# The seam between the first and second SAGE pass of a graph network: the last turn moved, norm and weights moved into the pass, memory laid out anew, graph 0 unpacked in one go

## The chip, the cores and the metric

One core of a Trainium2 chip runs the whole program in one launch. The metric is device time in microseconds, the median of several runs. Times inside the program are counted from the start of the profiled span. Engines are named as in the profile: PE (TensorE matmul), PEld (its weight loads), DVE (VectorE), ACT (ScalarE), POOL (GpSimd), SP (the engine that issues most DMAs here).

## The reference: what is computed

Sixteen graphs (B = 16) of 1024 nodes with 128 features each, and one adjacency matrix per graph.

```
x = layernorm(x + gated_graph_network(x, adj))        # layer 0: four rounds of aggregation and a GRU cell
adj_d = dilate(adj)                                   # row by row, drops some neighbours
# layer 1: three SAGE passes, each over all 16 graphs, with a batch norm over all graphs between them
def sage(x, Wr, Wx, b):
    agg = adj_d @ x / max(deg, 1)
    out = agg @ Wr + x @ Wx + b
    return out / max(norm(out), 1e-12) * mask
h1 = bn(relu(sage(x,  Wr1, Wx1, b1)))
h2 = bn(relu(sage(h1, Wr2, Wx2, b2)))
h3 = bn(relu(sage(h2, Wr3, Wx3, b3)))
x  = layernorm(x + concat(h1, h2, h3) @ Wl + bl)
```

The batch norm takes mean and variance over all 16 graphs. So pass two cannot form its weights before the last graph of pass one is through: the norm's scale is folded into the weights of the next pass, its shift into a bias row.

## The kernel before

Layer 0 and the dilation run up to about 1275 us, pass one (class Sage, function first) from there to 1704, pass two (second) to about 1949, pass three (third) and the end (last) to 2125.5.

**How a pass is staged.** A graph's work is cut into slots, 16 in pass one (slot, L1735) and 8 in pass two (slot_second, L1930). In each slot the code issues instructions for several graphs on all engines; the order of the code is the order on each engine, since the passes stand in a manual schedule. A graph's 1024 nodes are two halves f = 0 and 1 of 512. For a half, PE forms the output from aggregated features and the features themselves (pass one: out_first, L1705, banks p_oa and p_ob; pass two: out_next, L1907, banks q_oa and q_ob); DVE scales and adds (scale_rows, L1415 and L1416); ACT takes squares for the row norm (squares, L1423 and L1424); DVE makes the normalised rows s_r (rows, L1444 to L1449); ACT and POOL split them into a high and a low part (split, L1464 and L1465); PE turns them, four transposes into a PSUM tile s_tr (turned, L1470), ACT copies the tile out to s_rt and DVE takes its statistics (turn_r, L1732 and L1733). PE also aggregates the split rows with the adjacency (pass one: agg, L1696, banks p_ag; pass two L1954, banks q_ag), ACT copies the sums out to s_ag (evict, L1702), and SP stores s_rt and s_ag to DRAM, from where the next pass loads them.

**The last slots of graph 15 in pass one.** The turns of the halves stand in slots 11 and 13, the aggregation of the second half's high and low part in slots 12 and 14, the stores of the turned halves in slots 13 and 15 (L1832). The PSUM pool p_ps1, in which s_tr lies, has one buffer for each name.

**The seam.** run (L2161) calls first; then weights(1) (L1350): batch_norm (L1326 to L1331: statistics joined on DVE, a square root on ACT, four small DVE steps), three scaled weights (L1334: wr2, and the two halves of wxp), the shift as columns of beta (L1361), three matrix products for six bias rows in the PSUM tile s_v6 (L1362 to L1364, two matmuls each) and their split into three bf16 parts in r6 (parts, L1341 to L1348, eight DVE steps). Then it opens the pool of the accumulator acc (one tile for all graphs) and the pool s_ahead with three tiles s_rho, which POOL sets to zero (L2172), and calls second. There SP loads graph 0 (load_layer, L1877 and L1878: the sums q_agi, the turned features q_xt, the rows s_rho; load_second, L1887: acc; load_bytes, L1892: the first half of the adjacency, one byte for each entry), stores the two s_ag of graph 15 (L1865), and the slots begin. The load of the second half's bytes stands in slot 3.

**Unpacking.** The adjacency of pass two is cast from bytes to the matmul's type before it is used (unpack, L1895): eight casts for a graph, of 128x1024 each, one in a slot, four for the first half (tile q_at0) and four for the second (q_at1), on POOL, ACT, POOL, DVE in turn (L1903 for ACT, L1905 for the others). They begin in slot 3 of a graph and end in slot 2 of the next.

Memory comes from pools in a stack: a pool that is opened takes the addresses that a closed one left.

Of the kernel before, what the change touches and what calls it, by code (L numbers as in the profile page):

```python
# [1206 lines left out]
class Sage:  # L1207
# [191 lines left out]
    def start_half(self, b):  # L1399

        acc = self.acc[:, b, 4:, :]
# [333 lines left out]
    def slot(self, b, t):  # L1735
# [36 lines left out]
        if True:  # L1772
# [25 lines left out]
            if t in (11, 13):  # L1798
                self.turn_r(0, b, t // 13, self.ps1)
# [25 lines left out]
        if True:  # L1825
# [5 lines left out]
            if t in (13, 15):  # L1831
                nc.sync.dma_start(self.rt[b, t // 15], g["rt", t // 15])  # L1832
# [17 lines left out]
    def second(self):  # L1850

        nc, tc = self.nc, self.tc
        with ExitStack() as c:
# [27 lines left out]
    def load_second(self, b):  # L1881
# [5 lines left out]
        nc.sync.dma_start(self.acc[:, b], self.x1[b])  # L1887
# [7 lines left out]
    def unpack(self, b, t):  # L1895
# [5 lines left out]
        e = "gpsimd scalar gpsimd vector".split()[t % 4]  # L1901
# [5 lines left out]
    def out_next(self, b, f, ps):  # L1907
# [3 lines left out]
        for i in range(4):  # L1911
            blk = slice(i * P, (i + 1) * P)
            nc.tensor.matmul(pa[:, i, :], g["agi"][:, f, blk], self.wr2, start=True, stop=True)  # L1913
        for i in range(4):
# [15 lines left out]
    def slot_second(self, b, t):  # L1930
        nc, g, p = self.nc, self.g.get(b), self.g.get(b - 1)
        acc = lambda b, f: self.acc[:, b, 4 * f:4 * f + 4, :]
        if b < B:
# [5 lines left out]
            if t == 3:  # L1939
# [41 lines left out]
        if t >= 3:  # L1981
            if b < B:
                self.unpack(b, t - 3)
        elif p is not None:
# [10 lines left out]
    def third(self):  # L1995

        nc, tc = self.nc, self.tc
        with ExitStack() as c:
# [10 lines left out]
            for i in range(len(units) + 5):  # L2009
# [34 lines left out]
                if i < len(units):  # L2044
                    g["ss", f] = self.shared_squares(g["o", f])
                    acc = self.acc[:, b, 4 * f:4 * f + 4, :]
# [5 lines left out]
    def last(self):  # L2052
        nc, tc, cst = self.nc, self.tc, self.cst
        with ExitStack() as c:
# [12 lines left out]
            def half(b, f):  # L2067
# [6 lines left out]
                pp, acc = self.banks[b][f], self.acc[:, b, 4 * f:4 * f + 4, :]  # L2074
# [7 lines left out]
            def finish(b, f):  # L2082
                pp, acc = self.banks[b][f], self.acc[:, b, 4 * f:4 * f + 4, :]
# [77 lines left out]
    def run(self):  # L2161
        tc, nc = self.tc, self.nc
        self.first()
        with tc.tile_pool(name="s_psw", bufs=1, space=PSUM) as ps:
            self.weights(1, ps.tile([6, C], F32, name="s_v6"))
        accp = self.ctx.enter_context(tc.tile_pool(name="s_acc", bufs=1))
        self.acc = accp.tile([P, B, NB, C], F32, name="s_acc")
        self.rt_kept = self.late[:, :HF]
        self.ahead = self.ctx.enter_context(tc.tile_pool(name="s_ahead", bufs=1))
        self.rhos, self.layers = [self.ahead.tile([P, N], BF, name=f"s_rho{i}") for i in range(3)], 0  # L2170
        for t in self.rhos:
            nc.gpsimd.memset(t, 0.0)  # L2172
# [102 lines left out]
```

## Time and profile before

| | us |
|---|---|
| median of 3 runs | 2126.41 |
| the runs | 2126.14, 2126.41, 2129.80 |
| the profiled execution | 2127.28 |
| its span, first to last instruction | 2125.5 |
| PE busy in the span | 2050.1 (96%) |
| DVE, POOL, ACT busy | 1782.1, 1351.5, 1304.0 |
| mean granted clock of TensorE | 0.992 |

Busy time is an average over stages. What is of interest here is one short stretch, and in such a stretch the chain of waits tells more than shares do: which instruction ended last, what released it, and so on back.

### The profile page before, as it was taken

To read this page: it belongs to the slowest core of one execution; us is meant where nothing else is said; L and a number is where in the kernel's file an instruction comes from. 1 tells how busy PE (TensorE), PEld (TensorE's weight loads), DVE (VectorE), ACT (ScalarE), POOL (GpSimd) and SP (SyncE) were. 2 spreads that over 40 slices of the span, in tenths; PEclk is the share of its full clock that TensorE was granted. 3 is DMA by queue.
4 is the path that set the end of the run, shared out by engine and by line. 5 is a ranking of instruction groups with operands and counts; after the bars stand their busy time and mean duration, and the time that the engine had idled before them with its cause. 6 is when DMAs were issued, how large, how long until landed. Compare 5 with 4: busy or idle time off the path is not lost.

```text
span 2125.5 us, 32964 instructions
## 1 busy us (share of the span) xinstructions
PE 2050.1 (96%) x10218; PEld 1435.8 (68%) x10219; DVE 1782.1 (84%) x4090; ACT 1304.0 (61%) x3127; POOL 1351.5 (64%) x1459
## 2 busy tenths in 40 slices
PE   7999999999999999999999998999999989999997
PEld 4566556665655666556655656888888778888875
DVE  4898998988998988998889997888888767776876
ACT  3657557567466566565665655776677645555756
POOL 5458558557558468467466557777777545565866
PEclk9999999999999999999999998999999999999998
DMA  8348356348447457546367337888788589996515
GB/s 254 89 105 251 92 129 219 79 121 243 92 109 231 89 142 207 103 136 199 77 207 174 77 117 267 300 293 294 292 290 293 180 309 341 343 339 209 161 41 161
DMA packets 234896, 406.68 MB, mean 191 GB/s; under 512 B 79058, under 2 KB 101236, under 8 KB 234708
## 3 DMA queue, kind: packets, MB, share of 16 engines
q1 hardware_dynamic: 190388, 285.17, 40.5%
q0 software_dynamic: 41616, 117.98, 20.8%
q8 instruction: 83, 1.36, 0.3%
q10 hardware_dynamic: 2704, 1.31, 0.2%
q14 instruction: 105, 0.86, 0.1%
HBM read 314.00 MB, written 109.25 MB: 199 GB/s over the span
## 4 chain that ended last, share of the span: by engine, by line
PE 66%; DVE 16%; ACT 5%; issue 5%; DMA 4%; POOL 3%; SPq 0%; ACTq 0%; DVEq 0%; POOLq 0%
PE h_g L1104 18%; PE h_g L1092 13%; PE p_ag L1696 11%; PE q_ag L1954 5%; PE q_ob L1916 5%; DVE f_rank L737 4%; PE q_oa L1913 3%; DVE f_a L729 2%; PE p_u L1607 2%; PE s_tr L1470 2%; DMA h_a<-in_adj_dram 1%; PE h_g L1038 1%; DVE f_x L894 1%; ACT s_junk L1423 1%; DVE h_r L1116 1%
## 5 line engine op out<-in xcount | busy, mean ns | idle before, releaser
L1104 PE MATMUL h_g<-h_ms,h_wi 128*128 128x512 f32 x768 | 392.2, 592 | 0.0
L737 DVE TENSOR_TENSOR_SCAN f_rank<-f_a,f_first,f_pd 128x1024 f16<-128x1024 bf16 x128 | 299.4, 2345 | 4.2
L1092 PE MATMUL h_g<-h_a,h_hi 128*128 128x512 f32 x1024 | 278.2, 413 | 0.4 <-DMA h_a<-in_adj_dram 0.2
L1104 PEld LDWEIGHTS h_g<-h_ms,h_wi 128*128 128x128 f32 x768 | 145.5, 190 | 184.3 <-issue 168.9
L1092 PE MATMUL h_g<-h_a,h_lo 128*128 128x512 f32 x1024 | 262.1, 393 | 0.1
L1627 POOL CAST p_b<-p_at 128x512 uint8<-128x512 f32 x256 | 208.0, 834 | 80.6 <-DVE p_at L1619 42.4
L1092 PEld LDWEIGHTS h_g<-h_a,h_hi 128*128 128x128 f32 x1024 | 190.1, 188 | 60.5 <-issue 22.0
L1092 PEld LDWEIGHTS h_g<-h_a,h_lo 128*128 128x128 f32 x1024 | 189.6, 188 | 39.2 <-DVE h_lo L1031 1.1
L1123 POOL TENSOR_TENSOR h_zh<-h_r,h_h 128x512 f32<-128x512 f32 x64 | 82.3, 1286 | 199.1 <-ACT h_r L1119 196.1
L1104 PE MATMUL h_g<-h_h,h_wh 128*128 128x512 f32 x384 | 198.1, 597 | 3.3 <-DVE h_r L1116 3.3
L1104 PE MATMUL h_g<-late,h_wh 128*128 128x512 f32 x384 | 198.1, 597 | 0.7 <-DVE h_r L1116 0.7
L1119 ACT ACTIVATE h_r<-h_r,h_bi 128x512 f32<-128x512 f32 x128 | 92.4, 722 | 150.1 <-DVE h_r L1118 150.1
L1124 POOL TENSOR_TENSOR h_zh<-h_z,h_zh 128x512 f32<-128x512 f32 x128 | 165.6, 1294 | 10.0
L1095 ACT COPY h_ms<-h_g 128x512 f32<-128x512 f32 x128 | 73.7, 576 | 149.0 <-PE h_g L1092 148.8
L1423 ACT ACTIVATE s_junk<-s_o 128x128 bf16<-128x128 f32 x256 | 76.1, 298 | 128.6 <-DVE s_o L1416 128.6
L910 ACT ACTIVATE f_u<-f_rank,f_q 128x128 f16<-128x128 f16 (+7 forms) x128 | 110.5, 867 | 69.9 <-DVE f_rank L850 68.8
L1123 POOL TENSOR_TENSOR h_zh<-h_r,late 128x512 f32<-128x512 f32 x64 | 94.5, 1476 | 57.1 <-ACT h_r L1119 56.9
L2185 DVE SCALAR_TENSOR_TENSOR p_a<-p_a 128x1024 bf16<-128x1024 f32 x96 | 128.9, 1343 | 0.0
L778 POOL TENSOR_SCALAR_AFFINE_SELECT f_both<-f_both 128x512 bf16<-128x512 bf16 x32 | 20.6, 642 | 164.6 <-DVE f_both L777 164.6
L1916 PE MATMUL q_ob<-s_wxp,q_xt 128*128 128x256 f32 x512 | 121.7, 381 | 0.0
L887 ACT ACTIVATE f_pd<-f_rank,f_q 128x128 f32<-128x128 f16 x128 | 59.1, 462 | 98.9 <-DVE f_q L701 95.7
L1619 DVE SCALAR_TENSOR_TENSOR p_at<-p_nr,p_u 128x128 fp32r<-128x128 bf16 (+1 forms) x192 | 102.8, 543 | 19.9 <-ACT p_at L1611 15.4
(314 smaller groups left out, 5184.5 us busy)
## 6 DMA issues: line engine op xcount, KB each, us to landing
h_a<-in_adj_dram POOLq DMA_DIRECT2D x128, 512.0 KB, 9.3
p_a<-in_adj_dram SPq DMA_DIRECT2D x96, 512.0 KB
f_a<-in_adj_dram POOLq DMA_DIRECT2D x128, 256.0 KB, 6.3
e_nr<-f_nr SPq DMA_DIRECT2D x128, 256.0 KB
p_nr<-e_nr SPq DMA_DIRECT2D x32, 1024.0 KB
s_at<-p_b SPq DMA_DIRECT2D x32, 512.0 KB
s_ag<-s_ag SPq DMA_DIRECT2D x64, 256.0 KB
q_agi<-s_ag SPq DMA_DIRECT2D x32, 512.0 KB
```

The source lines that it names most:

```text
L737: nc.vector.tensor_tensor_scan(out, a, other[:, 0, 0:1].to_broadcast([P, N]), start, op0=ALU.add, op1=ALU.bypass)
L910: nc.scalar.activation(u[:, :n1], rank[:, g, :n1], AF.Abs, bias=q[:, 1, g:g + 1], scale=q[:, 0, g:g + 1])
L1092: nc.tensor.matmul(pm[f], part[:, j, :], st.adj[j][:, half[f]], start=(j == 0 and n == 0), stop=(j == NB - 1 and n == 1))
L1104: nc.tensor.matmul(pg, lhs, rhs, start=(i == 0), stop=(i == len(mm) - 1))
L1123: aid.tensor_tensor(d, r, h, ALU.subtract)
L1124: aid.tensor_tensor(d, z, d, ALU.mult)
L1619: self.nc.vector.scalar_tensor_tensor(g["at", f][:, j, :low], v[:, j, c0:c0 + low], 0.0, pu[:, :low], op0=ALU.is_lt, op1=ALU.is_lt)
L1627: self.nc.gpsimd.tensor_copy(g["b", f][:, j, :], g["at", f][:, j, :].bitcast(F32))
L1696: self.nc.tensor.matmul(pa, hi[:, j, :], at[:, j, :], start=(start and n == 0), stop=(stop and n == len(js) - 1))
L1916: nc.tensor.matmul(pb[:, i], g["xt"][:, f, blk], self.wxp, start=(i % 2 == 0), stop=False)
L1954: nc.tensor.matmul(p["pa", f], part[:, j, :], p["at", f][:, j, :], start=(t in (1, 4) and j == 0), stop=(t in (2, 5) and j == NB - 1))
L2185: nc.vector.scalar_tensor_tensor(junk, a, 0.0, a, op0=ALU.is_gt, op1=ALU.not_equal, accum_out=bad[:, c:c + 1])
```

## The change

- In pass one, for graph 15 alone, the turn of the second half moves from slot 13 to slot 12, ahead of that slot's aggregation; the stores of the turned halves move from slots 13 and 15 to slots 12 and 13.
- Right after that turn stands second_weights: batch norm, scaled weights and beta. wr2 is scaled as soon as the scale is there; beta's memset and copies go from DVE to POOL.
- The bias rows (three products and their split) are formed in pass two, in the first out_next, between the matmuls into q_oa and those into q_ob; their PSUM tile is one of s_tr.
- The pool s_ahead opens before that of acc; acc is 16 tiles, not one. In second four tiles (two q_rl, two s_rt) are taken from the pool q_wk ahead of all others and not used at that place; later tiles of these names take their turn.
- The first s_rho is set to zero before graph 0's loads, the other two between POOL's casts.
- The bytes of both halves of graph 0 are loaded at once, and its eight casts stand ahead of the slots: the first half's four on ACT, the second's four on POOL. The slots of graph 0 issue no casts.

```diff
-    def batch_norm(self, l):
+    def batch_norm(self, l, early=False):
...
         nc.vector.tensor_mul(ab[:, 0:1], ab[:, 0:1], vt[:, 3 * l + 1:3 * l + 2])
+        if early:
+            self.scaled(self.wr2, self.wr[:, l + 1, :], l)
         nc.vector.tensor_mul(mv[:, 0:1], mv[:, 0:1], ab[:, 0:1])
...
     def weights(self, l, v):
-        if l:
+        if l == 1:
+            beta = self.beta
+        elif l:
             self.batch_norm(l - 1)
...
+        if l:
             nc.tensor.matmul(v, beta[:, 0, :], self.wr[:, l, :], start=True, stop=False)
...
+    def second_weights(self):
+        nc, l = self.nc, 1
+        self.beta = beta = self.small.tile([C, 2, 6], F32, name="s_beta")
+        nc.gpsimd.memset(beta, 0.0)
+        self.batch_norm(0, True)
+        for i in range(2):
+            nc.gpsimd.tensor_copy(beta[:, i, 3 * i:3 * i + 3], self.ab[0][:, 1:2].to_broadcast([C, 3]))
+        self.scaled(self.wxp[:, 0, :], self.wx[:, 1, :], 0)
+        self.scaled(self.wxp[:, 1, :], self.wl[:, 0, :], 0)
...
-            if t in (11, 13):
-                self.turn_r(0, b, t // 13, self.ps1)
+            slots = (11, 12) if b == B - 1 else (11, 13)
+            if t in slots:
+                self.turn_r(0, b, slots.index(t), self.ps1)
+                if (b, t) == (B - 1, 12):
+                    self.second_weights()
...
-            if t in (13, 15):
-                nc.sync.dma_start(self.rt[b, t // 15], g["rt", t // 15])
+            slots = (12, 13) if b == B - 1 else (13, 15)
+            if t in slots:
+                nc.sync.dma_start(self.rt[b, slots.index(t)], g["rt", slots.index(t)])
...
+            for i in range(2):
+                self.wk.tile([P, NB, C], FR, name="q_rl")
+                self.wk.tile([C, HF], F32, name="s_rt")
+            nc.gpsimd.memset(self.rhos[0], 0.0)
             self.load_second(0)
-            self.load_bytes(0, 0)
+            for f in range(2):
+                self.load_bytes(0, f)
             for f in range(2):
                 nc.sync.dma_start(self.ag[B - 1, f], last["ag2"][f])
+            for f in range(2):
+                for t in range(4):
+                    self.unpack(0, 4 * f + t, ("scalar", "gpsimd")[f])
+                    if f == 1 and t in (1, 3):
+                        nc.gpsimd.memset(self.rhos[t // 2 + 1], 0.0)
...
             nc.tensor.matmul(pa[:, i, :], g["agi"][:, f, blk], self.wr2, start=True, stop=True)
+        if self.layers == 1:
+            self.weights(1, self.ps1.tile([P, 4, P], F32, name="s_tr")[:6, 0, :])
...
-            if t == 3:
+            if t == 3 and b:
                 self.load_bytes(b, 1)
...
-            if b < B:
+            if 0 < b < B:
                 self.unpack(b, t - 3)
-        elif p is not None:
+        elif b > 1:
             self.unpack(b - 1, t + 5)
...
         self.first()
-        with tc.tile_pool(name="s_psw", bufs=1, space=PSUM) as ps:
-            self.weights(1, ps.tile([6, C], F32, name="s_v6"))
-        accp = self.ctx.enter_context(tc.tile_pool(name="s_acc", bufs=1))
-        self.acc = accp.tile([P, B, NB, C], F32, name="s_acc")
-        self.rt_kept = self.late[:, :HF]
         self.ahead = self.ctx.enter_context(tc.tile_pool(name="s_ahead", bufs=1))
         self.rhos, self.layers = [self.ahead.tile([P, N], BF, name=f"s_rho{i}") for i in range(3)], 0
-        for t in self.rhos:
-            nc.gpsimd.memset(t, 0.0)
+        accp = self.ctx.enter_context(tc.tile_pool(name="s_acc", bufs=1))
+        self.acc = [accp.tile([P, NB, C], F32, name=f"s_acc{b}") for b in range(B)]
+        self.rt_kept = self.late[:, :HF]
         self.second()
```

More of the change, by code (lines that the diff above doesn't have):

```diff
@@ L1399, in start_half @@
     def start_half(self, b):
-        acc = self.acc[:, b, 4:, :]
+        acc = self.acc[b][:, 4:, :]
         self.head_banks(b)
@@ L1886, in load_second @@
         g = self.g[b]
-        nc.sync.dma_start(self.acc[:, b], self.x1[b])
+        nc.sync.dma_start(self.acc[b], self.x1[b])
     def load_bytes(self, b, f):
@@ L1893, in load_bytes, with unpack @@
             self.g[b]["b", f] = t
-    def unpack(self, b, t):
+    def unpack(self, b, t, e=None):
         nc, g, f, j = self.nc, self.g[b], t // 4, 2 * (t % 4)
@@ L1900, in unpack @@
         dst, src = g["at", f][:, j:j + 2, :], g["b", f][:, j:j + 2, :]
-        e = "gpsimd scalar gpsimd vector".split()[t % 4]
+        e = e or "gpsimd scalar gpsimd vector".split()[t % 4]
         if e == "scalar":
@@ L1931, in slot_second @@
         nc, g, p = self.nc, self.g.get(b), self.g.get(b - 1)
-        acc = lambda b, f: self.acc[:, b, 4 * f:4 * f + 4, :]
+        acc = lambda b, f: self.acc[b][:, 4 * f:4 * f + 4, :]
         if b < B:
@@ L2045, in third @@
                     g["ss", f] = self.shared_squares(g["o", f])
-                    acc = self.acc[:, b, 4 * f:4 * f + 4, :]
+                    acc = self.acc[b][:, 4 * f:4 * f + 4, :]
                     self.late = acc, pb[:, :, 1, :], acc
@@ L2073, in half @@
                         self.head_banks(b)
-                pp, acc = self.banks[b][f], self.acc[:, b, 4 * f:4 * f + 4, :]
+                pp, acc = self.banks[b][f], self.acc[b][:, 4 * f:4 * f + 4, :]
                 for i in range(4):
@@ L2082, in finish @@
             def finish(b, f):
-                pp, acc = self.banks[b][f], self.acc[:, b, 4 * f:4 * f + 4, :]
+                pp, acc = self.banks[b][f], self.acc[b][:, 4 * f:4 * f + 4, :]
                 for i in range(4):
```

## The prediction

> **What bounds the kernel now.** I read the span in stages first: busy time of each engine in each stretch. Columns: stretch and its length, then busy us (instructions) of PE, PEld, DVE, ACT, POOL, then the granted clock, the DMA share and GB/s.
>
> ```profile
> 1305.80:1704.00 398.20, 391.50 (x2930) 322.20 (x2929) 322.42 (x841) 272.40 (x784) 282.32 (x300) 1.00 0.76 274
> 1704.00:1723.80 19.80, 12.70 (x75) 10.41 (x74) 13.04 (x34) 6.19 (x24) 6.00 (x6) 0.91 0.83 300
> 1723.80:1949.00 225.20, 222.16 (x1262) 189.06 (x1263) 170.37 (x324) 124.88 (x409) 131.21 (x94) 1.00 0.92 321
> ```
>
> The two passes are bound by PE (391.5 of 398.2 us and 222.2 of 225.2). The seam between them is the 19.8 us from 1704.0 to 1723.8, in which no engine is full: there a chain decides. So I read the chain of work that ended last in that stretch (start, length, what):
>
> ```profile
> 1704.16 0.83 POOL s_rho L2172
> 1704.99 3.54 DMA q_agi<-s_ag
> 1708.54 0.49 issue
> 1709.03 2.05 PE q_oa L1913 x8
> 1711.07 2.25 PE q_ob L1916 x8
> ...
> 1713.59 0.70 DVE s_o L1416
> ...
> 1714.44 1.29 ACT s_junk L1423 x8
> ...
> 1720.68 1.63 POOL q_rl L1465
> 1722.31 1.45 POOL q_at L1905
> ```
>
> The reader sees, after the last aggregation of pass one: load of graph 0's sums, its output matmuls, then norm, and at the end POOL's cast of the adjacency bytes, for which PE stands still. Last I read the timeline of single engines for the steps that the change touches:
>
> ```profile
> 1699.22 0.60 PE L1470 MATMUL s_tr<-ident,s_r 128*128 128x128 f32 x4
> 1699.65 2.11 PE L1696 MATMUL p_ag<-p_at,p_rh 128*128 128x512 f32 x8
> ...
> 1723.81 2.18 PE L1954 MATMUL q_ag<-q_at,q_rh 128*128 128x512 f32 x8 [1.85 <-POOL q_at L1905]
> ```
> ```profile
> 1699.86 0.59 ACT L1732 COPY s_rt<-s_tr 128x512 f32<-128x512 f32 x1 [0.26 <-PE s_tr L1470]
> ...
> 1720.93 1.05 ACT L1903 CAST q_at<-q_b 128x1024 fp32r<-128x1024 uint8 x1
> 1721.88 0.62 ACT L1464 CAST q_rh<-s_r 128x512 fp32r<-128x512 f32 x1
> ```
>
> PE waits 1.85 us for POOL before pass two's first aggregation, at 1723.81; its transposes before that ended at 1721.32 + 0.63 = 1721.95, and matmuls overlap by some 0.1, so without this wait it would start at 1721.85. **The prize is 2.0 us**, 0.1% of the kernel, plus whatever the start of the chain gives.
>
> Order and waits of all that follows the first two graphs of pass two, and of all before pass one's last slots, are the same in both programs, up to one memset of 0.95 us (an s_rho) that moves to the start of pass one's last graph, on POOL, which later idles 11.19 us before 1695.47: nothing. So only the seam counts, and PE then runs without a break (14.10 busy of 14.10 us in the stretch after 1723.80), and a shift of the aggregation at 1723.81 goes to the end undiminished. All times below are on the clock of the profile of before.
>
> **Last turn sooner.** Both turns of graph 15 now stand next to each other on PE. They share one PSUM buffer (pool p_ps1 has one), and the second must wait until ACT has copied out the first: transposes 1699.22, copy 1699.86 to 1700.45, so the second turn starts at 1700.55. Before, an aggregation of 1.9 us filled this gap and began at 1699.65. PE stands 0.9 us, and the last aggregation ends at 1704.94, not 1704.04. Statistics, norm and scaled weights come sooner (second copy at 1701.15, not 1702.23), but they were not on the path: wr2 was ready at 1706.08, q_agi landed at 1708.54.
>
> **Memory laid out anew.** In the built program the first load of graph 0 on SP still waits for the last aggregation matmul of pass one, for the store of the second turn and for the rest of what the closed pools held, as before; the new addresses do not change that list. Before, that store ended the wait (issued 1702.85, last of its landing events 1704.85, load issued 1704.99). Now the aggregation does: 1704.94, and 0.13 from PE's end to the next queue (POOL's first memset followed by that much): load at 1705.07, 0.1 later. It moves everything below by 0.1.
>
> **Weights in the pass.** q_agi lands at 1708.64. Before, q_oa started at 1709.03 and not at 1708.6, since PE also waited for DVE's second step on the bias rows (L1342, 1708.54 to 1708.82). That wait goes: q_oa at 1708.75, 0.3 sooner. But the six bias matmuls, which ran in the wait (1707.28 to 1708.19), now stand behind q_oa on PE, and DVE's eight splitting steps behind them. q_oa's eight take 1.84 at half clock (1709.03 to 1710.87), six more at 0.23 make 1.38: 1711.97, result 1712.2; the split took 1708.23 to 1710.20, 1.97: 1714.2; then L1415 (it was at 1711.27, hidden) and, 0.79 behind it as at 1717.01 and 1717.80, L1416 at 1715.0. It was at 1713.59: **1.4 us later**, if nothing else is later still.
>
> **Graph 0 unpacked at once.** Something is. Four casts of q_at0 stand on ACT ahead of graph 0's squares, and each engine takes its instructions in order: at 1721.17 the input of q_rh was ready, yet it began at 1721.88, when the cast before it was through. The casts wait for the byte load, SP's fifth; its landing events end at 1713.72 (the loads before it at 1708.54, 1709.83, 1712.38), now 1713.82. Casts follow each other by 0.95 (1720.93, 1721.88), four are 3.8: the squares start at 1717.65, not at 1714.44, **3.2 us later**. This covers the 1.4 above. POOL's four casts and two memsets begin when the second byte load lands (1.34 behind, 1715.2): 4 x 1.25 + 2 x 0.95 = 6.9, done at 1722.1, before q_rl can start (1723.9): hidden, by 1.8 us.
>
> From the squares to the first aggregation nothing changes but the casts that are gone, so 1721.85 + 3.2 = 1725.05, against 1723.81. **Sum: 2.0 won, 3.2 lost, 1.2 us slower.**
>
> **What else moves on SP.** The second byte load now stands ahead of the two s_ag stores and of graph 1's loads, 1.34 us each. q_agi of graph 1 lands at 1717.8 (was 1716.36), q_xt at 1719.15; PE asks for them at 1721 and 1722, since graph 0 is late: no cost, 2.9 to 3 us of cover. rho of graph 1 waits for its memset, now behind two casts on POOL (1715.2 + 2.5 + 0.95 = 1718.65), and acc and the bytes of graph 1 stand behind it; PE needs rho at about 1723.7 and the bytes were first read at 1735.30: covered.
>
> **The clock.** Two more stretches, same columns:
>
> ```profile
> 1704.00:1709.00 5.00, 0.94 (x7) 0.39 (x7) 3.44 (x14) 0.77 (x2) 2.87 (x3) 0.96 0.64 215
> 1709.00:1712.00 3.00, 2.98 (x11) 2.82 (x12) 1.82 (x6) 0.00 (x0) 0.00 (x0) 0.50 0.78 255
> ```
>
> After 5 us with 0.94 us of PE work the granted clock is 0.50 until 1712, and 1.00 from there on. It now falls likewise, so that is no difference. PE has one new hole, 1717.7 to 1720.4. If the clock fell there too, the price by rows is that of the first time: q_oa 2.05 for 1.11, q_ob 2.46 for 1.89, 1.5 us. The hole in pass one before 1695.44 (2.00 idle) left the clock at 1.00, which is the nearest row; I take nothing and keep 1.5 for the range.
>
> [...]
>
> **Rivals.** (a) *The gain comes.* If the byte load landed by 1711.6, the casts would be hidden and the 1.4 us of the weights' path would remain: 2.0 - 1.4 = 0.6 us faster. At best the weights cost nothing either, 2.0 faster, 2124.4. For it: DMA moved only 299 GB/s from 1710 to 1712.4 and 411 later. Against: four loads of 512 KB stand ahead in one queue. (b) *Slower, by the byte load.* Behind it now follows another of 512 KB in place of two of 256. If the DMA engines served neighbours at the same time, it would land with the next (1715.15): 1.3 more, 2128.9; with all up to q_xt of graph 1 (1719.15): 5.3 more, 6.5 slower, 2132.9. Every microsecond of its landing is one of the kernel's; from 1716.8 on it is over 0.2% in all. Against: with the same queue behind it the landings came one by one, 1.3 us apart. (c) *The clock falls again*: 1.2 + 1.5 slower, 2129.1. (d) That the new layout doesn't free the first load is part of the forecast; were it freed up to the landing of the second turn's store (some 1703.8, as the store is issued 1.1 sooner), all would be 1.2 sooner and the kernel as fast as before.
>
> **How the numbers follow.** The profiled execution took 2127.28 (span 2125.5 and 1.8 around it), 0.9 above the median 2126.41 of runs from 2126.14 to 2129.8. 2127.28 + 1.2 = 2128.5 for a profiled execution, 2126.41 + 1.2 = 2127.6 for the median. Chances: forecast 0.68, (a) with (d) 0.16, (b) 0.10, (c) 0.06. What a measurement can tell from no change is about 0.2%, 4.25 us. Faster by that lies beyond the best of (a) and needs what I don't see: 0.04. Slower by that is most of (b) and (c) together with part of it: 0.12. Within: 0.84. The range goes from the best of (a), 2124.4, to (c) with the scatter of the runs, 2129.8; it leaves out the far part of (b).
>
> **What would show it.** In the profile after: PE idle for 0.9 before the second turn, released by ACT's copy; the first q_agi load issued only after the last aggregation of pass one has ended; four ACT casts at 1713.8 to 1717.6 and the squares of graph 0 right behind; PE's first q_ag with no wait for POOL, 20.1 us after the last p_ag's end, and not 19.8. Wrong: squares that start before 1716, a first load before the last aggregation ends, or a second stretch at half clock.

## The result, and the profile after

| | before | after |
|---|---|---|
| median (lowest to highest), 13 runs each, side by side | 2127.42 (2125.92 to 2131.54) | 2132.27 (2130.24 to 2134.50) |
| the profiled execution and its span | 2127.28, 2125.5 | 2132.76, 2130.7 |
| mean granted clock of TensorE | 0.992 | 0.989 |
| end of pass one's last aggregation to first q_ag | 19.8 | 21.9 |

The ratio after to before is 1.0017, 95% interval 1.0009 to 1.0024: 3.6 us slower by the ratio, where 1.2 was forecast, and a median above the range. Timed a second time (after_again below), the same two kernels gave 1.0003 (0.9994 to 1.0012). The kernel after had nearly the same median as at first, 2132.47; it was the kernel before that moved, to a median of 2130.41, with single runs from 2126.32 to 2135.56. So two things have to be explained: what the change costs, and why one pair of kernels gives two answers.

The timeline of PE in the kernel after, over the same place as the prediction's (columns: start, duration, engine, line, operands; in brackets the idle time before it and what ended it):

```profile
1695.64 3.14 PE L1711 MATMUL p_ag<-p_at,p_rh 128*128 128x512 f32 x8 [1.99 <-ACT p_rh L1479]
...
1702.28 0.66 PE L1485 MATMUL s_tr<-ident,s_r 128*128 128x128 f32 x4 [0.68 <-ACT s_rt L1747]
...
1710.32 2.05 PE L1942 MATMUL q_oa<-s_wr,q_agi 128*128 128x128 f32 x8 [3.73 <-DMA q_agi<-s_ag]
...
1722.92 0.66 PE L1485 MATMUL s_tr<-ident,s_r 128*128 128x128 f32 x4 [2.82 <-DVE s_r L1464]
1723.52 1.91 PE L1942 MATMUL q_oa<-s_wr,q_agi 128*128 128x128 f32 x8
1725.22 2.84 PE L1947 MATMUL q_ob<-s_wxp,q_xt 128*128 128x256 f32 x8
```

The last turn's wait for ACT's copy is there (0.68), the wait for POOL before q_ag is gone, and in its place PE waits 2.82 for graph 0's rows. ACT's timeline says why; the squares stand right behind the four casts:

```profile
1715.95 3.89 ACT L1932 CAST q_at<-q_b 128x1024 fp32r<-128x1024 uint8 x4 [8.73 <-DMA q_b<-s_at]
1719.74 0.30 ACT L1438 ACTIVATE s_junk<-s_o 128x128 bf16<-128x128 f32 x1
```

The stretches of the prediction's first fence, on the clock of after (same columns as below): from the last p_ag to the first q_ag, and from there to the last graph of pass two.

```profile
1706.59:1728.49 21.90, 14.37 (x76) 11.46 (x75) 10.33 (x26) 8.95 (x26) 8.29 (x10) 0.84 0.72 255
1728.49:1953.69 225.20, 222.15 (x1267) 189.20 (x1265) 170.17 (x323) 123.96 (x408) 127.88 (x91) 1.00 0.92 322
```

The first is 2.1 us longer than before, at a mean clock of 0.84 for 0.91; in the second nothing has changed (PE 222.15 busy for 222.16). So far the forecast. What it did not have is in the durations: q_oa takes 1.91 at 1723.52 and q_ob 2.84, where they took 1.16 and 1.89 before, and p_ag at 1695.64 takes 3.14 for 2.11. The view of stretches shows the granted clock there (stretch, length, busy time of PE, PEld, DVE, ACT, POOL, the clock, DMA share, GB/s; the cuts lie 3.41 us apart, on the grid of this profile's clock changes at 1696.42, 1699.83, 1723.73 and 1727.14):

```profile
1693.01:1696.42 3.41, 1.42 (x9) 1.11 (x8) 2.98 (x8) 1.36 (x7) 0.76 (x1) 1.00 0.00 0
1696.42:1699.83 3.41, 3.41 (x9) 2.64 (x8) 3.27 (x6) 1.99 (x10) 0.53 (x1) 0.50 0.00 0
...
1720.32:1723.73 3.41, 0.81 (x6) 0.64 (x6) 2.27 (x5) 0.90 (x7) 2.69 (x3) 1.00 0.66 246
1723.73:1727.14 3.41, 3.41 (x13) 3.05 (x13) 2.36 (x6) 2.64 (x12) 0.75 (x1) 0.50 0.16 65
```

In both pairs a stretch in which PE works little (1.42 and 0.81 us of 3.41) is followed by one at half clock. The first pair lies in pass one, where the change moves nothing: the hole of 2.0 us is in both kernels.

The spans differ by 5.15. Cut at three events of PE, that is: 0.2 up to the hole in pass one; 1.6 from there to the last graph's first turn (5.37 for 3.78, the clock); **2.8 in the seam, from that turn to the fourth q_oa of pass two, that of graph 1's second half (31.20 for 28.43)**; and 0.6 behind it (398.47 for 397.88). The expectations below call this q_oa the third; the lengths that they give are measured to the fourth, 1727.65 in the first profile of before.

### The profile page after: what moved, and what is told of

The parts are those of the page before. It is cut to its first block, busy times and chain, and to the rows that moved or that the text cites. A ratio compares the mean times of both kernels' runs of the same rounds, so it can differ in the third digit from the quotient of the medians.

```text
span 2130.7 us, 32959 instructions
## 1 busy us (share of the span) xinstructions
PE 2054.1 (96%) x10219; PEld 1438.8 (68%) x10219; DVE 1781.0 (84%) x4085; ACT 1306.3 (61%) x3129; POOL 1351.0 (63%) x1462
```

## The experiments

The theory after the result: four casts on ACT stand ahead of graph 0's squares and cost more than POOL's wait did, as forecast; and the hole that they open in PE lets the clock fall. The rival: half-clock stretches come and go in either kernel, and what differs beyond the forecast is chance. Others: the earlier turn, the bias rows behind q_oa, or the layout lose the time.

All results together. The seam is the length just defined, from the run's one profile. "Falls" are half-clock stretches between 1693 and 1735, 3.41 us long where nothing else is said. Left out is the one that begins at 1706 to 1710, behind the wait for the first load, in every kernel but e10 and e12; it lasts 6.83 us and not 3.41 in before_again, e1, e6 and e8.

| run | ratio to before (95%) | seam, us | falls |
|---|---|---|---|
| before, first profile | | 28.43 | none |
| before_again | | 31.21 | behind the hole in pass one; behind the wait for POOL |
| after, first profile | 1.0017 (1.0009, 1.0024) | 31.20 | behind the hole in pass one; behind the casts |
| after_again | 1.0003 (0.9994, 1.0012) | 31.08 | behind the casts |
| e1_turn13 | 1.0007 (0.9999, 1.0016) | 30.96 | as the first profile of after |
| e2_casts_in_slots | 1.0014 (1.0005, 1.0023) | 31.55 | behind the wait for POOL |
| e3_pool_casts | 0.9986 (0.9976, 0.9995) | 28.38 | none |
| e4_rows_early | 1.0011 (1.0002, 1.0020) | 31.41 | behind the casts (6.83 us long) |
| e5_pool_rows | 0.9988 (0.9979, 0.9997) | 28.28 | behind a new hole of 2.12 |
| e6_old_layout | 1.0006 (0.9997, 1.0015) | 31.14 | behind the casts |
| e8_warm | 1.0009 (0.9999, 1.0019) | 29.89 | none |
| e9_split | 0.9995 (0.9986, 1.0004) | 26.30 | none |
| e10_ahead | 0.9976 (0.9967, 0.9985) | 24.18 | none, nor the one behind the load |
| e11_before_filled | 0.9990 (0.9981, 0.9999) | 28.44 | none |
| e11_again | 0.9995 (0.9984, 1.0006) | 28.39 | none |
| e13_after_filled | 1.0001 (0.9992, 1.0011) | 30.02 | none |
| e12_best | 0.9969 (0.9957, 0.9981) | 24.62 | at 1706.36, behind the wait for DVE's split of the bias rows |

### The kernels unchanged, a second time

> The kernel before, unchanged, profiled a second time, to see which stretches at half clock are the kernel's and which come and go. Theory (the half-clock stretch 1723.7 to 1727.1 of the kernel after is made by its new 2.6 us hole in PE; that of 1696.4 to 1699.8 in pass one comes and goes with the moment at which windows of the clock begin): no stretch at half clock after 1712 in the seam, one at 1708.6 to 1712.0; one at 1696 to 1700 may or may not be there. Rival (both stretches come and go in either kernel): the list differs from that of the first profile, also in pass two's first microseconds.

> The kernel after, unchanged, profiled a second time and timed in five rounds against the one before. Theory: ratio 1.0012 to 1.0024; the squares of graph 0 again right behind four ACT casts, the new hole in PE of 2.6 us again there, and with it the half-clock stretch behind it; that in pass one may be missing, which takes 1.6 us off the profiled time. Rival (the clock falls by chance only): no half-clock stretch after 1714 in this profile and the span 3 us shorter, 2127.5.

before_again, one run of 2131.24, settles for the rival in one point: the kernel before has both falls too. Its timeline of PE:

```profile
1695.20 3.47 PE L1696 MATMUL p_ag<-p_at,p_rh 128*128 128x512 f32 x8 [2.00 <-ACT p_rh L1464]
...
1726.48 3.59 PE L1954 MATMUL q_ag<-q_at,q_rh 128*128 128x512 f32 x8 [1.86 <-POOL q_at L1905]
```

Both aggregations stand behind the same holes as in the first profile (2.00 and 1.85 there) and take 3.47 and 3.59, not 2.11 and 2.18. The view of stretches, for before_again and then for the first profile of before, at the wait for POOL:

```profile
1722.90:1726.31 3.41, 1.26 (x10) 0.73 (x9) 3.24 (x7) 2.27 (x4) 2.96 (x2) 1.00 0.54 123
1726.32:1729.73 3.41, 3.25 (x8) 2.57 (x9) 1.20 (x2) 2.74 (x11) 3.41 (x5) 0.50 1.01 384
```

```profile
1722.26:1725.67 3.41, 1.86 (x8) 1.43 (x9) 2.49 (x4) 1.58 (x10) 3.41 (x4) 1.00 0.97 313
1725.67:1729.08 3.41, 3.41 (x21) 2.99 (x20) 1.68 (x5) 2.14 (x4) 2.29 (x3) 1.00 1.04 404
```

The holes are equally long. In before_again 1.69 us of the hole and the idle 0.46 before the transposes ahead of it lie in one window of 3.41 us; PE is busy for 1.26 of it, and the next window runs at 0.50. In the first profile 1.55 us of the hole lie in the window and the idle 0.47 before the transposes in the one before it; PE is busy for 1.86 us, and the clock stays. The edges lie differently against the program from run to run: taken from the moments at which the clock changes, their phase in the 17 profiles is anywhere from 0.2 to 3.4 us. Of the 2.8 us by which this seam is longer than the first one, 1.4 are this fall; the other 1.3 come from the longer half-clock stretch behind the first load (the first q_ob takes 3.62 for 2.46). after_again had the fall behind the casts again and none in pass one; its span, 2131.1, was not shorter by 1.6, as I had expected: the hole in pass one itself came 1.65 us later in it (1697.29 for 1695.64), and the end of the program took longer.

### One part undone: casts, turn, rows, layout

**e2_casts_in_slots** puts the casts of graph 0 back into the slots, and the load of the second bytes into slot 3.

```diff
-            for f in range(2):
-                for t in range(4):
-                    self.unpack(0, 4 * f + t, ("scalar", "gpsimd")[f])
...
-            if t == 3 and b:
+            if t == 3:
                 self.load_bytes(b, 1)
...
-            if 0 < b < B:
+            if b < B:
                 self.unpack(b, t - 3)
-        elif b > 1:
+        elif p is not None:
...
```

> The kernel after, with graph 0's casts back in its slots, and the load of the second half's bytes back in slot 3. Theory (the block of four casts on ACT ahead of the squares costs 3.1 us, and the hole it opens in PE another 1.5 by the clock): the squares start no longer behind casts, the second half-clock stretch is gone, PE waits for POOL's cast again (2 us), and the bias rows are bare: 1.4 us later than in the kernel before. Against the kernel before +1.0 to +1.5 us (ratio 1.0005 to 1.0007), against the kernel after -1 to -3. Rival (the loss is in the earlier turn and the weights moved into the pass): no faster than the kernel after, ratio 1.0015 to 1.0024.

Half right. The fall behind the casts was gone and the wait for POOL back (1.85), but with a fall of its own behind it (q_ag 3.56 for 2.18). Ratio 1.0014, seam 31.55: no faster than after. Against the first profile of before, graph 0's squares start 1.6 us later behind the first turn (16.81 for 15.22; the last turn's stall and the bare bias rows, where 1.4 was expected), and the fall adds the rest, 1.5. So e2 is spared the price of the casts and pays for the rows and for another fall in its place.

**e3_pool_casts** has four casts at once on POOL, none on ACT; the second half's stay in the slots.

```diff
-            for f in range(2):
-                for t in range(4):
-                    self.unpack(0, 4 * f + t, ("scalar", "gpsimd")[f])
...
+            for t in range(4):
+                self.unpack(0, t, "gpsimd")
...
-            if 0 < b < B:
+            if b < B and (b or t == 7):
                 self.unpack(b, t - 3)
```

> The kernel after, with the four casts of graph 0's first half all on POOL ahead of the slots, none on ACT, and those of its second half back in the slots. Theory (ACT's in-order queue is what lost the gain): ACT's squares wait for DVE alone, PE has no wait for POOL's cast before its first aggregation (POOL's four casts, 5 us, end by 1719), and what is left is the bias rows behind q_oa (+1.4) against 2.0 won: -0.6 us against the kernel before, ratio 0.9996 to 0.9999; 3 to 5 us less than the kernel after. Rival (casts are not what the seam waits for, or the clock falls whatever the casts do): 1.0010 or more.

Here both holes are gone, and it is the first kernel faster than before, 0.9986. PE has one wait of 1.22 us left, for the split of the bias rows on DVE (the two steps of L1350 take 1.38 us here, beside POOL's casts, and 0.71 in after), and from there no wait over half a microsecond up to q_ag:

```profile
1717.07 0.38 PE L1949 MATMUL q_ob<-s_r,s_rho 128*128 128x128 bf16 x4 [1.22 <-DVE s_r L1350]
...
1721.29 0.66 PE L1485 MATMUL s_tr<-ident,s_r 128*128 128x128 f32 x4 [0.44 <-DVE s_r L1464]
1721.88 1.16 PE L1941 MATMUL q_oa<-s_wr,q_agi 128*128 128x128 f32 x8
1722.88 1.89 PE L1946 MATMUL q_ob<-s_wxp,q_xt 128*128 128x256 f32 x8
...
1725.84 2.09 PE L1984 MATMUL q_ag<-q_at,q_rh 128*128 128x512 f32 x8
```

It is faster than expected (-3 for -0.6 us), though against the first profile of before, which has no fall, the seam is no shorter: what it saves is probably the falls. That is read from one profile of each, and not shown.

**e1_turn13**: turn, norm and weights back in slot 13, the stores in 13 and 15.

```diff
-            slots = (11, 12) if b == B - 1 else (11, 13)
+            slots = (11, 13)
...
-                if (b, t) == (B - 1, 12):
+                if (b, t) == (B - 1, 13):
                     self.second_weights()
...
-            slots = (12, 13) if b == B - 1 else (13, 15)
+            slots = (13, 15)
```

> The kernel after, with the last turn, norm and weights back in slot 13 and the stores of the turned halves in 13 and 15. Theory (the earlier turn gains nothing: PE loses 0.7 to 0.9 us waiting for the one PSUM buffer, and the first load starts sooner by as much): within 0.4 us of the kernel after, and no wait of PE for ACT between the two turns; the first load issued some 0.9 us after the last aggregation, not 0.1. Rival (the stall of PE is what the change lost): 0.7 to 0.9 us faster than the kernel after.

The theory held: from the first turn to the end of the last aggregation 4.73, for 5.58 after; from there to q_oa 4.74, for 3.73 to 3.92. What the earlier turn wins at the load it loses on PE.

**e4_rows_early** forms the bias rows at the end of first, not in the first out_next.

```diff
                 for t in range(16):
                     self.slot(b, t)
+            self.weights(1, self.ps1.tile([P, 4, P], F32, name="s_tr")[:6, 0, :])
...
-        if self.layers == 1:
-            self.weights(1, self.ps1.tile([P, 4, P], F32, name="s_tr")[:6, 0, :])
```

> The kernel after, with the bias rows of pass two formed at the end of pass one, before graph 0's loads are waited for. Theory (the rows behind q_oa are covered by the cast block on ACT): q_ob, L1416's like and s_o are 1.4 us sooner, the squares start where they did, and the time is that of the kernel after within 0.4 us. Rival (the rows behind q_oa are on the path): 1.0 to 1.4 us faster than the kernel after.

DVE's last step before the squares ended at 1714.37, yet they began behind the casts, at 1717.78: the rows are covered by the casts, and the time is that of after. The hole in PE grew to 4.68.

**e6_old_layout** undoes the layout: one accumulator tile, opened first, and no tiles taken ahead.

```diff
+        whole = accp.tile([P, B, NB, C], F32, name="s_acc")
+        self.acc = [whole[:, b] for b in range(B)]
...
-                self.wk.tile([P, NB, C], FR, name="q_rl")
-                self.wk.tile([C, HF], F32, name="s_rt")
```

> The kernel after with the memory laid out as before: the accumulator one tile, opened ahead of the pool of the rho rows, and without the four tiles taken first. Theory (the new layout frees nothing): first load issued 0.1 us behind the last aggregation, as in the kernel after, and the time within 0.5 us of its, ratio to before 1.0003 to 1.0017. Rival (the layout frees a load, or a buffer, earlier): the first load or one of its followers is issued later, and 1 us or more is lost against the kernel after.

First load 0.07 us behind the last aggregation (1705.30, 1705.23), ratio 1.0006. The loads behind it are issued up to 0.5 us later, since the one of s_rho waits for its memset (the bytes 2.23 behind the last aggregation, 1.79 in after), but the casts start no later (8.83 behind it): the layout changes nothing in the time.

### The clock alone

**e8_warm** fills the hole behind the casts with matmuls whose results are not used.

```diff
                 self.out_next(b, t // 3, self.ps1)
+                if (b, t) == (0, 3):
+                    junk = self.ps1.tile([C, HF], F32, name="q_ag0")
+                    for i in range(12):
+                        nc.tensor.matmul(junk, self.cst["ident_b"], self.mask48[:, :HF], start=True, stop=True)
```

> The kernel after, with twelve matmuls of 128x512 in bf16 (some 2.6 us, their results are not used) on PE behind graph 0's second output, where PE stands idle for the casts. Theory (a window of 3.41 us in which PE is busy for less than about half makes the next one run at half clock, so the hole of 2.5 to 2.8 us behind the cast block costs 1.5 us more than the wait itself): PE's busy share in that window goes over 0.9, no half-clock stretch between 1714 and 1732, q_oa of graph 1 takes 1.16 and not 1.55 to 1.91, q_ob 1.89 and not 2.84 to 3.22, and from the end of pass one's last aggregation to the first q_ag 20.2 us, not 21.8. Against the kernel after -1.5 us. Rival (the half-clock stretches come at times that have nothing to do with this hole): the stretch is there all the same, or the 21.8 us stay.

By its profile the theory held: no fall, q_oa 1.06, q_ob 1.89, seam 29.89 for 31.1. The ratio, 1.0009, does not show it. In this profile the stretch from the fourth q_oa to the end is 2.2 us longer than in the first profile of before (400.13 for 397.88), with a half-clock stretch at 1942.88, between passes two and three, that after does not have. One profile cannot say how often that comes.

**e11_before_filled** does the same to the kernel before, at both holes; e11_again is the same kernel in a later set.

```diff
                     if t == 9:
                         g["pb", f] = bank()
+                        if f == 0 and b == B - 1:
+                            for i in range(8):
+                                nc.tensor.matmul(g["pb", f], self.cst["ident_b"], self.mask48[:, :HF], start=True, stop=True)
...
                 part = p["rh"] if t in (1, 4) else p["rl"]
+                if (b, t) == (1, 1):
+                    for i in range(8):
+                        nc.tensor.matmul(p["pa", f], self.cst["ident_b"], self.mask48[:, :HF], start=True, stop=True)
```

> The kernel before, with eight matmuls of 128x512 in bf16 (1.8 us, results not used) in each of two places where PE stands idle for 1.85 to 2.0 us: ahead of the last graph's first p_rh in pass one, and ahead of the first q_ag of pass two. Neither hole is longer or shorter for what follows; only the clock can be. Theory (a hole of 1.9 to 2 us makes the next 3.41 us run at half clock when most of it falls into one window, which happened in 3 of 10 profiles at the first place and in 1 of 2 of the kernel before at the second): no half-clock stretch behind either place in this profile, the median 1 to 2 us below that of the kernel before (ratio 0.9991 to 0.9996), and fewer of its runs above 2131. Rival (half-clock stretches do not depend on PE's load here): same median, or a stretch at one of the two places.

> The kernel before with both holes filled, again, beside the kernel after filled. Theory: as the first time, ratio to before 0.9986 to 0.9994, no half-clock stretch behind either hole. Rival (the first run's gain was scatter): 0.9996 to 1.0004.

Nothing of the kernel's own work starts sooner by itself: PE's filler ends before the awaited operand comes (timeline of PE in e11_before_filled):

```profile
1721.76 1.89 PE L1958 MATMUL q_ag<-s_mask,ident_b 128*128 128x512 bf16 x8
1723.78 2.18 PE L1960 MATMUL q_ag<-q_at,q_rh 128*128 128x512 f32 x8
```

Still the kernel with sixteen useless matmuls was timed faster: 0.9990 (0.9981 to 0.9999), in the second set 0.9995 (0.9984 to 1.0006). The first interval excludes no change, the second does not; neither profile has a fall behind the two places.

**e13_after_filled** has both holes of after filled (eight in pass one, nine behind the second output), and stands beside e11_again.

> The kernel after, with matmuls whose results are not used in both of its holes: eight in pass one's, nine (2 us) behind graph 0's second output. Compared with the next run, the kernel before with both of its holes filled, it shows what the change costs when the clock does not fall in either. Theory (1.2 us for the seam by casts against POOL's wait, as forecast, and 0.8 to 1.0 at the end of pass three, which six profiles of kernels with the casts on ACT show and no other): 1.2 to 2.2 us more than the kernel before filled; ratio to before 0.9995 to 1.0002; from the start of the first turn to the third q_oa 29.4 to 29.9 us, against 28.4. Rival (the change's loss is the clock's alone): the two filled kernels within 0.5 us.

Ratios 1.0001 and 0.9995, medians 2130.93 and 2128.45; seam 30.02 and 28.39 to 28.44. Without these falls the change costs **1.6 us in the seam**. Of what I expected at the end of pass three (0.8 to 1.0), its profile shows 0.5.

### What a better seam needs

**e5_pool_rows** is e3 with the rows of e4.

> Casts of graph 0's first half all on POOL and none ahead of the squares on ACT, and the bias rows formed at the end of pass one, in one kernel. Theory: both steps add up once the cast block is gone: from the end of pass one's last aggregation to the first q_ag 17.7 to 18.0 us (19.8 in the first profile of before, 19.05 with the casts alone on POOL), no half-clock stretch behind the one at 1710; against the kernel before -3 to -5 us, ratio 0.9977 to 0.9986. Rival (something else, the byte load or POOL's casts, is next): 19 us, and no faster than with the casts on POOL alone.

It missed: ratio 0.9988 and seam 28.28, no better than e3. DVE's timeline shows a new wait, inside two of its steps:

```profile
1716.46 0.18 DVE L1459 RECIPROCAL s_ss<-s_ss 128x4 f32<-128x4 f32 x1 [1.12 <-ACT s_ss L1439]
1716.67 0.81 DVE L1460 SCALAR_TENSOR_TENSOR s_ss<-s_ss,mask 128x4 f32<-128x4 f32 x1
1717.52 1.47 DVE L1464 SCALAR_TENSOR_TENSOR s_r<-s_o,s_ss 128x512 f32<-128x512 f32 x1
```

They take 0.17 and 0.69 in e9 below; POOL's four casts run from 1714.47 to 1718.45. PE then stands for 2.12, is busy for 1.29 us of that window of 3.41, and the clock falls to 0.50 at 1719.38.

**e9_split** leaves two casts on POOL and puts two on ACT behind graph 0's first squares.

```diff
                 pp = self.chain(b, f)
+                if (b, t) == (0, 0):
+                    for i in (2, 3):
+                        self.unpack(0, i, "scalar")
```

> The kernel with the bias rows formed at the end of pass one, and graph 0's first four casts divided: two on POOL at once, two on ACT behind the squares of its first half (in the run before this one all four were on POOL, and beside them DVE's step L1460 took 0.81 us for 0.17 and L1464 1.47 for 0.69). Theory (POOL's casts hold DVE up on the path, 1.4 us, and the hole of 2.1 us that this leaves in PE lets the clock fall for another 1.3): L1460 takes 0.17 to 0.2 and L1464 0.7, PE's hole before the first transposes of graph 0 is 0.5 to 0.8 us, no half-clock stretch from 1714 to 1735, from the start of the last graph's first turn to the third q_oa 25.6 us for 28.3; ratio to before 0.9970 to 0.9980. Rival (DVE's long steps have another cause): they stay, and the time is that of all four on POOL, 0.9988.

In the profile the mechanism held: POOL's casts end at 1716.13, and the same two steps of DVE are short.

```profile
1716.30 0.17 DVE L1460 SCALAR_TENSOR_TENSOR s_ss<-s_ss,mask 128x4 f32<-128x4 f32 x1
1716.50 0.69 DVE L1464 SCALAR_TENSOR_TENSOR s_r<-s_o,s_ss 128x512 f32<-128x512 f32 x1
```

No fall, seam 26.30 (25.6 expected), two microseconds less than in e5. The ratio missed: 0.9995, not 0.9970 to 0.9980. As in e8, the rest of the span is 2.0 us longer than in the first profile of before (399.87), with a half-clock stretch at 1941.00. Why the runs as a whole did not gain stays open.

**e10_ahead** is e9 with graph 0's first loads put into the pool s_ahead, whose addresses no pool of pass one holds to its end. They are then issued before pass one is over: that of q_agi at 1659.61, with the last aggregation ending at 1704.49 (in after the load follows the aggregation, at 1706.67).

```diff
-            self.load_second(0)
+            self.g[0] = self.load_layer(0, self.ahead)
+            nc.sync.dma_start(self.acc[0], self.x1[0])
```

> The same, and graph 0's sums and turned features are loaded into tiles at addresses that no pool of pass one holds, so that these loads need not wait for the last aggregation. Theory (the 3.7 us for which PE waits between the passes are the wait of the first load for memory): those loads are issued before pass one ends, PE's first q_oa follows the last aggregation by 1.5 to 2.5 us (it then waits for the weights or for the bias rows), the accumulator and bytes land some 2.5 us sooner; no half-clock stretch at 1710, as no window stands empty. Against the kernel with the loads behind: -2.5 to -4 us; ratio to before 0.995 to 0.9965. Rival (the loads would land no sooner, behind other transfers in their queue): within 1 us of it.

q_oa follows the last aggregation by 2.34 (before 4.99), now behind DVE's splitting of the rows, at full clock:

```profile
1706.82 1.13 PE L1943 MATMUL q_oa<-s_wr,q_agi 128*128 128x128 f32 x8 [0.88 <-DVE s_part L1345]
```

Ratio 0.9976, against 0.9995 of e9: four microseconds, where 2.5 to 4 were expected. The seam, 24.18 for 26.30, accounts for two of them.

**e12_best** adds eight filler matmuls in pass one's hole, as in e11.

> The fastest kernel so far (bias rows at the end of pass one, casts divided, graph 0's first loads ahead) with eight matmuls whose results are not used in pass one's hole. Theory: the half-clock stretch behind that hole, which comes in about one run of three, goes, so the median falls by 0.3 to 0.7 us: ratio to before 0.9970 to 0.9976. Rival (no such stretches in this kernel): the same as without them, 0.9976, or slower if the matmuls push the first p_rh.

Ratio 0.9969 (0.9957 to 0.9981), median 2124.52 beside 2129.56 of before: the fastest, 6.6 us by the ratio. Whether the filler adds to e10 the overlapping intervals do not say. The seam of the two kernels is not safe from falls either. In both, PE's first q_oa follows the last aggregation by 2.33 to 2.34 us, with little but the bias products in between. In e10 the clock stayed; in e12 the window that ends at 1706.36 holds 2.00 us of PE's work, and the next ran at half clock:

```profile
1706.57 3.48 PE L1949 MATMUL q_ob<-s_wxp,q_xt 128*128 128x256 f32 x8
```

In e10 this step took 1.89. So that e10's profile shows no fall there looks like luck: the rest that can bring it is still there, though its expectation had the fall gone for good.

## Why the prediction was wrong

**Last turn sooner: right.** Forecast 0.9 lost on PE; measured 5.58 - 4.82 = 0.76. q_oa behind the last aggregation by 3.81; measured 3.73 to 3.92. e1 confirms that the two cancel.

**Layout: right.** The first load waits for the last aggregation (issued 0.08 behind it), and e6 changes nothing.

**Weights in the pass: right.** The rows cost PE's q_ob a wait (0.55), covered by the casts; e4. Where nothing covers them, in e2, the squares start 11.23 behind the last aggregation; the forecast's 1.4 makes 10.9.

**Casts ahead of the squares: right.** In e13 the casts begin 8.88 us behind the last aggregation, forecast 8.88; the squares 12.67, forecast 12.71. In after_again, e4, e6 and e8 the casts begin 8.83 to 8.90 behind it. In the first profile of after it is 9.36 (squares 13.15), half a microsecond later; the 1.3 or more of rival (b) was never seen.

**"POOL's four casts and two memsets ... hidden, by 1.8 us": wrong.** They were done in time for q_rl, but they hold DVE up. In after L1460 takes 0.64, in e13 0.94, against 0.17; the same is seen as 1.43 for 0.69 in L1464 of e4. DVE in e13, and then POOL:

```profile
1719.18 0.18 DVE L1459 RECIPROCAL s_ss<-s_ss 128x4 f32<-128x4 f32 x1 [2.40 <-ACT s_ss L1439]
1719.39 0.94 DVE L1460 SCALAR_TENSOR_TENSOR s_ss<-s_ss,mask 128x4 f32<-128x4 f32 x1
1720.37 0.69 DVE L1464 SCALAR_TENSOR_TENSOR s_r<-s_o,s_ss 128x512 f32<-128x512 f32 x1
```
```profile
1718.30 2.02 POOL L1937 CAST q_at<-q_b 128x1024 fp32r<-128x1024 uint8 x2
1720.26 0.95 POOL L1897 MEMSET s_rho<- 128x1024 bf16 x1
```

L1460 ends at 1720.33, when POOL's cast ends at 1720.32. So it is in all eight profiles in which L1460 is long at this place (after, after_again, e1, e5, e6, e8, e10, e13): it ends within 0.03 us of the end of a cast of POOL. The memset behind the cast holds nothing up: beside it L1464 takes its 0.69.

That is 0.5 to 0.8 us on the path: from the squares to the first q_ag e13 takes 8.04, where the sum had 7.40, and e9, whose DVE steps are short, takes 7.40. It makes up the seam's 1.6 against the 1.2 of the sum. L1460 and L1464 read two operands, L1459 one; in e5, beside POOL's casts, they take 0.81, 1.47 and 0.18. The profile of before has the same three steps in pass one, as L1445, L1449 and L1444, beside POOL's cast L1627. L1445 takes 0.31 to 0.36 in all 15 cases in which a cast runs beside it, and 0.16 to 0.17 in the other 51; L1449 takes 1.05 in the one case in which casts cover it whole, and 0.69 to 0.70 in the 14 in which they cover half of it; L1444 takes 0.16 to 0.18 with a cast beside it or without. Why the three differ is not shown: no run varies the operands.

**"The hole in pass one ... left the clock at 1.00, which is the nearest row; I take nothing": this is the step that failed**. One row was taken as a property of the hole, when it was one draw. The same hole cost 1.6 us in 3 of the 13 profiles in which it was not filled. Behind the casts the clock fell in 5 of 5 unfilled profiles (rival (c), which I gave 0.06; the prediction's own sign of being wrong, a second stretch at half clock), and behind the wait for POOL in 2 of 3. Behind the casts it costs 0.9 to 1.4 us of the seam (30.96 to 31.41 for the 30.02 of e13). So the fall is no price of the change alone: before has one, too, in the very wait that the change removes. The forecast had missed both, on both sides.

**"So only the seam counts": wrong as well.** At the end of pass three, from the start of its last q_oa to that of the first product with the accumulator (q_oa from s_acc), PE takes 6.20 to 6.22 us in the six other profiles with the cast block of after, 5.68 in e13 and 5.17 to 5.19 in the ten without it. So the change costs 0.5 to 1.0 us there too, which the forecast had at nothing. PE waits there for POOL's rows (1.6 us in sum in after, 0.7 in before); what shifts the engines against each other 300 us behind the seam was not tried, and stays open.

**The level of the runs.** The sum was set on 2126.41, the median of three. In the five sets, of which the first holds those three runs, the same kernel had medians of 2127.42, 2130.41, 2129.66, 2130.68 and 2129.56, in 135 runs from 2124.62 to 2135.56. A range of 5.4 us around a median of three runs was narrower than the kernel's own scatter. Falls of the clock may explain part of it: by their clock records, the profiles hold between 23.9 and 37.5 us at half clock ahead of the stretch in which the program ends, and a stretch of 3.41 us costs up to 1.6 (5.37 for 3.78 in pass one of after). The last four sets ran on three different chips; how much of the level is the chip's was not tried.

Thus of the 5.15 between the two profiles 1.6 are pass one's fall (chance), 1.6 the forecast's loss with POOL's part (30.02 - 28.43), 1.2 the fall behind the casts (31.20 - 30.02), and 0.8 lie before and behind (0.2 and 0.6, in which the 1.0 at the end of pass three is partly made up elsewhere). By its terms the change costs 1.6 in the seam, some 1.2 by the fall and 0.5 to 1.0 at the end of pass three: 3.3 to 3.8 against a kernel before without falls. That is near the 3.6 of the first timing; in the second, 0.6, it was the kernel before that was slower, and why its level moved from 2127.42 to 2130.41 is not shown.

## What to carry to other kernels

Here a wait of 1.85 us for POOL was removed, and one of 2.82 came in its place, since the squares now stood behind the moved casts on ACT; see what is next in the queue that takes the work, and which steps of other engines run beside it (L1460 took 0.94 for 0.17 beside POOL's cast in e13), before pricing the move at the old wait. PE's hole of 2.0 us in pass one cost 1.6 more by the clock in 3 of 13 profiles, and nothing more in the other ten; judge such an edit by whether it leaves any hole, and compare profiles with the falls counted apart. Where the effect sought is a tenth of a per cent, take the level of the kernel before from many runs, not from three.

## What the runs showed of the hardware

Half clock followed windows in which PE did a good deal of work: 1.42 us of 3.41 (after, 1693.01), 2.00 us (e12, the window that ends at 1706.36). In the clock records of before and after the changes lie whole multiples of 3.41 us apart (half-clock stretches of 3.41, 6.83 and 10.24 in after). From the moments at which the clock changed, I laid such a grid over each of the 17 profiles and summed PE's busy time in each window between 1685 and 2070 us that ran at full clock with less than 0.9 busy. Of 43 windows with a busy share under 0.45, all were followed by a half-clock window; of 164 with 0.50 or more, three were, at 0.57 to 0.59, while five others between 0.56 and 0.58 were not. What brings full clock back the busy share does not say: at half clock a window with 0.84 of PE's time (e11_again, 1706.92) was followed by full clock, one with 1.00 (e8_warm, 1707.34) by another at half clock.
